# Sums of attention weights by queries, reciprocals transposed to features, and a fused mask and maximum in the first of four blocks

## The chip, the cores and the metric

The kernel runs on one core of a Trainium2 chip, in float32 throughout. The metric is the device time of one execution in microseconds. Five engines work side by side, each through its own instruction queue in order: TensorE (PE; its weight loads are shown as PEld), VectorE (DVE), ScalarE (ACT), GpSimd (POOL) and SyncE (SP), which issues the DMAs. Engines wait for each other through semaphores. Matrix products land in PSUM, of which the kernel uses eight banks of 128 x 512 words in rotation; everything else lies in SBUF.

## The reference, cut to what matters

Four blocks follow each other on x of shape (2, 2048, 256): a grouped-query attention block with its feed-forward part, two layers of a local-attention block, a gated block, and a linear layer with ternary weights. Each is added to its own input. The change lies in the attention of the first block:

```
q = (h @ Wq + bq) in 16 heads of 16;  k, v = 4 heads of 16, each shared by 4 query heads
q, k = rope(q), rope(k)
scores = q k^T / sqrt(16)
valid = (col <= row) & (row - col < 64)      # causal window of 64
attn = softmax(where(valid, scores, -1e9))
x = x + concat_heads(attn @ v) @ Wo + bo
```

Then comes the feed-forward part of the same block, with a layer norm, a product to 1024 features, a gelu and a product back to 256.

## The kernel before, in words

The 4096 rows are 32 tiles of 128 queries, in 8 groups of 4 tiles. A tile goes through the first block in four consecutive steps of a schedule: tile t is projected in step t, scored in step t+1, attended in step t+2 and multiplied by Wo in step t+3. So one step holds four tiles at different stages: `p` (project), `q` (scores), `a` (attend) and `o` (output). The function `step_a` writes out the order by hand, and each engine executes its own instructions in just that order: nothing is reordered.

Groups add work to certain steps. `m` normalises the rows of the group that comes next (line 169, step 4g-2). `n` takes its statistics one step earlier (lines 145 to 159), and in the same steps GpSimd adds the output bias to another group's rows (line 206). `f` prepares the feed-forward part of a finished group (statistics on VectorE, a power on GpSimd at lines 135 and 137, normalised rows at line 197 on VectorE, then eight transposes at line 214 on TensorE); it falls on steps 7, 11, 15, 19, 23, 27, 31 and 35. `e` (last statistics) normalises the finished rows. From step 8 on, the feed-forward products fill the steps: `fill(0)` and `fill(1)` issue two pieces each, either hidden features (lines 555 and 561) or outputs (lines 566 and 573). Steps 2 to 7 attend tiles without such pieces.

The attention of one tile: TensorE makes the scores of 16 heads for a window of 128 keys, 32 small products into four banks (line 449). VectorE adds the mask, a bank of four heads in one operation (`mask`, line 459), takes the maxima of eight heads at a time (`maxima`, line 468), and GpSimd subtracts them (line 469). ScalarE takes the exponents of all 16 heads in one instruction (line 472). In the next step TensorE transposes the weights so that keys lie on partitions (line 479), ScalarE copies them out (line 487), and `values` multiplies them: by V (line 499), and a second time by a matrix of zeros and ones, `one48` (line 506), which gives, for every feature of every head, the sum of that head's weights. `take_values` then takes the reciprocal of 256 columns of sums (line 515) and multiplies (line 516). The program's `ps` tiles are PSUM banks, and nearly all SBUF tiles are slices of one tensor called `room`.

Of the kernel before, what the change touches and what calls it, by code (L numbers as in the profile page):

```python
# [12 lines left out]
ALU = mybir.AluOpType  # L13
AX = mybir.AxisListType
# [3 lines left out]
P = 128  # L18
# [6 lines left out]
KC = D // P  # L25
# [4 lines left out]
AH, AKV, AHD, ADFF, AWIN = 16, 4, 16, 1024, 64  # L30
AKW = AWIN + P
AG = AH // AKV
# [13 lines left out]
def kernel(ctx: ExitStack, tc: tile.TileContext, I: dict, out: bass.AP):  # L46
    nc = tc.nc
    uid = [0]

    def T(pool, shape, tag, bufs=None):  # L50
        uid[0] += 1
        kw = {} if bufs is None else {"bufs": bufs}
        return pool.tile(shape, F32, tag=tag, name=f"{tag}_{uid[0]}", **kw)

    def load(t, src):
        nc.sync.dma_start(out=t, in_=src)
# [9 lines left out]
    small = ctx.enter_context(tc.tile_pool(name="small", bufs=3))  # L66
# [3 lines left out]
    ident = T(const, [P, P], "ident")  # L70
# [9 lines left out]
    def bank():  # L80
        return T(ps, [P, 512], "ps")

    def bank4():
        return bank().rearrange("p (t c) -> p t c", c=P)
# [140 lines left out]
    def load_qkv(l):  # L225
        w = {}
        w["wqkv"] = T(wB, [P, KC, 3 * BIN], "wqkvB")
        load(w["wqkv"], I["L0_ffn_wqkv"][l].rearrange("(k p) n -> p k n", p=P))
        return w
# [42 lines left out]
    wa = Region(HIGH + 5184, W_A, 2, low_tags)  # L272
    ca = wa
# [83 lines left out]
    VW, NVW = 3 * AHD, 4  # L357
# [3 lines left out]
    for i in range(NVW):  # L361
# [3 lines left out]
        for lst, name in ((vown, "vown"), (vmid, "vmid")):  # L365
            lst.append(T(ca, [P, AKV, VW], f"{name}{i}", 1))
            nc.gpsimd.memset(lst[i], 0.0)
    one48 = T(ca, [P, VW], "one48", 1)
    nc.gpsimd.memset(one48, 0.0)
    nc.gpsimd.memset(one48[:, AHD : 2 * AHD], 1.0)  # L370

    class TileA:

# [15 lines left out]
        def take(self):  # L389
            t, tl = self.t, self.t % TPS  # L390
            qkv = self.qkv = T(wa, [P, 384], "qkv")
            nc.vector.tensor_add(qkv, self.pm[:, :384], bqkvA)

            vo = vown[t % NVW]
            nc.gpsimd.tensor_copy(
                vo[:, :, AHD : 2 * AHD], qkv[:, 320:384].rearrange("p (g d) -> p g d", d=AHD)
            )
            load(vmid[t % NVW][64:128], vo[0:64])
            if tl < TPS - 1:
                load(vmid[(t + 1) % NVW][0:64], vo[64:128])  # L400

            nh, hf = AH + AKV, AHD // 2
            qk = self.qk = qkv[:, 0:320].rearrange("p (h d) -> p h d", d=AHD)
            sin = ropeA[:, tl, 1, :].unsqueeze(1)
            t2 = self.t2 = T(wa, [P, nh, AHD], "t2")
            nc.gpsimd.tensor_mul(
                t2[:, :, 0:hf], qk[:, :, hf:AHD], sin[:, :, 0:hf].to_broadcast([P, nh, hf])
            )
            nc.gpsimd.tensor_mul(
                t2[:, :, hf:AHD], qk[:, :, 0:hf], sin[:, :, hf:AHD].to_broadcast([P, nh, hf])  # L410
            )
            cos = ropeA[:, tl, 0, :].unsqueeze(1)
            self.t1 = T(wa, [P, nh, AHD], "t1", 1)
            nc.vector.tensor_mul(self.t1, qk, cos.to_broadcast([P, nh, AHD]))
# [38 lines left out]
                        )  # L453

        def mask(self, g):
            if g == 0:
                self.S = T(wa, [P, AKV * AG, P], "S")
            m = maskA0 if self.first else maskA
            nc.vector.tensor_add(
                self.S[:, g * AG : (g + 1) * AG, :],  # L460
                self.scs[g].rearrange("p (c w) -> p c w", c=AG),
                m.unsqueeze(1).to_broadcast([P, AG, P]),
            )

        def maxima(self, half):
            Sh = self.S[:, half * 2 * AG : (half + 1) * 2 * AG, :]
            mc = T(small, [P, 2 * AG], "mxA")
            nc.vector.reduce_max(mc, Sh, axis=AX.X)
            nc.gpsimd.tensor_sub(Sh, Sh, mc.unsqueeze(2).to_broadcast([P, 2 * AG, P]))  # L469

        def exponents(self):
            nc.scalar.activation(self.S, self.S, AF.Exp, scale=1.0 / AHD**0.5)

        def weights_to_keys(self):
            self.pts = []
# [13 lines left out]

        def values(self):  # L490

            pm = self.po = bank().rearrange("p (s k q) -> p s k q", s=2, k=2)
            vw = (vmid[self.t % NVW], vown[self.t % NVW])
            for b in range(2):
                q = slice(64 * b, 64 * b + 64)
                for e in range(2):
                    c0 = 0 if e else AHD
                    for g in range(AKV):
                        nc.tensor.matmul(
                            pm[32 * g : 32 * g + 32, 0, :, q], vw[b][:, g, c0 : c0 + 32],  # L500
                            self.PT[g // 2][:, g % 2, :, e, q], start=e == 0, stop=e == 1,
                        )
            for e in range(2):
                c0 = 0 if e else AHD
                for g in range(AKV):
                    nc.tensor.matmul(
                        pm[32 * g : 32 * g + 32, 1, :, :], one48[:, c0 : c0 + 32],
                        self.PT[g // 2][:, g % 2, :, e, :], start=e == 0, stop=e == 1,
                    )

        def take_values(self):
            pm = self.po
            self.oT = T(wa, [P, KC, P], "oT")
            rd = T(wa, [P, KC, P], "rdA", 1)
            nc.vector.reciprocal(rd, pm[:, 1])
            nc.vector.tensor_mul(self.oT, pm[:, 0], rd)

        def output(self):
            pm = self.pm = bank()
# [76 lines left out]
    for g in range(NG):  # L596
# [4 lines left out]
        s = GT * (g + 1) + 3  # L601
# [13 lines left out]
    def step_a(todo):  # L615
        p = a = q = o = n = m = f = e = None
        for (g,) in todo.get("load", ()):
            if g:
                groups_a[g] = GroupA(g)
        if "project" in todo:  # L620
            (t,) = todo["project"][0]
            if t == GT:
                weights.update({**load_qkv(0), **load_wo(0), **load_ffn(0)})
            p = tiles_a[t] = TileA(t, groups_a[t // GT])
        if "scores" in todo:
            q = tiles_a[todo["scores"][0][0]]
        if "attend" in todo:
            a = tiles_a[todo["attend"][0][0]]
        if "output" in todo:
            o = tiles_a.pop(todo["output"][0][0])  # L630
        for (g,) in todo.get("residual", ()):
            ffns_a[g] = FfnA(groups_a[g])
        if "statistics" in todo:
            n = groups_a[todo["statistics"][0][0]]
        if "normalise" in todo:
            m = groups_a[todo["normalise"][0][0]]
        if "prepare" in todo:
            f = ffns_a[todo["prepare"][0][0]]
        if "finish" in todo:
            e = ffns_a.pop(todo["finish"][0][0])  # L640

        def fill(place):

            rest = []
            for g, what, i in todo.get(f"fill{place}", ()):
                x = ffns_a[g]
                if what == "hidden":
                    rest.append(lambda x=x, i=i, r=x.hidden(i): x.take_hidden(i, r))
                else:
                    rest.append(lambda x=x, i=i, r=x.output(i): x.take_output(i, r))  # L650
            return rest

        if q:
            q.scores()
            q.mask(0)
            q.mask(1)
        if p:
            p.project()
            p.take()
        if q:  # L660
            q.mask(2)
        if p:
            p.rotate()
        if q:
            q.maxima(0)
            q.mask(3)
            q.maxima(1)
        pieces = fill(0)
        if a and not pieces:
            a.weights_to_keys()  # L670
            a.take_weights()
        for r in pieces:
            r()
        if n:
            n.statistics()
        if f:
            f.statistics()
        if e:
            e.last_statistics()
        if p:  # L680
            p.to_features()
            p.take_features()
        if a and pieces:
            a.weights_to_keys()
            a.take_weights()
        for r in fill(1):
            r()
        if m:
            m.normalise()
        if f:  # L690
            f.normalise()
        if e:
            e.last_normalise()
        if a:
            a.values()
            a.take_values()
        if o:
            o.output()
            o.add_output()
        if q:  # L700
            q.exponents()
        if m:
            m.to_features()
            m.residual()
        if f:
            f.to_features()
        for (g,) in todo.get("bias", ()):
            groups_a[g].add_bias()
# [491 lines left out]
    for l in range(BL):  # L1200
# [9 lines left out]
        for g in range(NG):  # L1210
            s = s0 + GT * (g + 1) + 3
# [511 lines left out]
```

## Time and profile before

| what | value |
| --- | --- |
| median of 3 runs | 2646.41 us (2644.96 to 2647.05) |
| time of the profiled execution | 2644.28 us |
| its span on the core | 2642.5 us |
| granted TensorE clock, mean | 0.99 |
| busy: PE, DVE, ACT, POOL | 97%, 61%, 45%, 38% |
| steps 0 to 34 of the first block | about 4 us to 507 us |

The page gives sums over the whole program, which has several stages with different limits. The first block takes the first fifth of it. A timeline of one engine lists its instructions in order of time: start, duration, engine, line, operation, and in brackets the idle time before it with its releaser. Durations of consecutive VectorE instructions overlap by some 0.08 us, so the distance from start to start, not the duration, says what one more instruction costs. The chain of work that ended last lists, for a stretch of time, the instructions that each instruction in turn was waiting for.

### The profile page before, as it was taken

How to read it: one execution, taken by the hardware profiler on the slowest of the kernel's cores; microseconds unless marked ns; L12 is line 12 of the kernel's file. 1: busy time of each engine (PE TensorE's matmuls, PEld its weight loads, DVE VectorE, ACT ScalarE, POOL GpSimd, SP SyncE). 2: the span in 40 equal slices, each digit the busy share in tenths (PEclk: the TensorE clock that was granted, in tenths of full speed). 3: DMA queues.
4: the chain of work that ended last, by engine and by line, in shares of the span. 5: the costliest groups of instructions: out<-in, count | busy, mean ns of one | idle time of the engine just before them, and what ended most of it. 6: DMA issues, size and time to landing. Idle time of an engine off the chain costs nothing.

```text
span 2642.5 us, 51312 instructions
## 1 busy us (share of the span) xinstructions
PE 2576.2 (97%) x20130; PEld 1645.9 (62%) x20130; DVE 1608.4 (61%) x4357; ACT 1199.7 (45%) x2507; POOL 995.4 (38%) x1237
## 2 busy tenths in 40 slices
PE   6899999998999999999999999999999999999998
PEld 4577777666666666666676676666544455445567
DVE  6878777567666766667666667774434335434344
ACT  3555555465666666756567666663500001500000
POOL 5565555545434544435444445542200002300011
PEclk8999999999999999999999999999999999999999
DMA  5001101111001011011310111101100000100000
GB/s 171 17 31 32 32 32 40 47 33 51 25 17 26 25 26 29 22 55 29 89 37 18 29 34 37 25 22 53 40 8 4 6 7 12 44 0 6 5 11 13
DMA packets 73169, 82.03 MB, mean 31 GB/s; under 512 B 18829, under 2 KB 57056, under 8 KB 72672
## 3 DMA queue, kind: packets, MB, share of 16 engines
q1 hardware_dynamic: 72928, 78.75, 10.6%
q8 instruction: 160, 2.62, 0.4%
q14 instruction: 81, 0.66, 0.1%
HBM read 44.20 MB, written 10.50 MB: 21 GB/s over the span
## 4 chain that ended last, share of the span: by engine, by line
PE 91%; DVE 4%; POOL 3%; issue 1%; DMA 0%; ACT 0%; SPq 0%; POOLq 0%; ACTq 0%; DVEq 0%
PE ps L1576 17%; PE ps L900 12%; PE ps L1154 10%; PE ps L1177 6%; PE ps L1500 4%; PE ps L566 4%; PE ps L555 4%; PE ps L1082 4%; PE ps L975 3%; PE ps L1053 2%; PE ps L1519 2%; PE ps L1488 2%; PE ps L1025 2%; PE ps L956 2%; PE ps L1478 2%; PE ps L479 2%
## 5 line engine op out<-in xcount | busy, mean ns | idle before, releaser
L1576 PE MATMUL ps<-room 128*128 128x512 f32 (+1 forms) x1152 | 463.2, 544 | 0.0
L1576 PEld LDWEIGHTS ps<-room 128*128 128x128 f32 x1152 | 217.8, 189 | 221.9 <-issue 214.7
L900 PE MATMUL ps<-room 128*128 128x512 f32 x768 | 347.4, 602 | 0.0
L1006 ACT ACTIVATE room<-room,shift,rn 128x192 f32<-128x192 f32 x512 | 276.0, 546 | 71.7 <-DVE shift L994 71.7
L921 POOL TENSOR_TENSOR room<-room 128x256 f32<-128x256 f32 x128 | 113.5, 887 | 500.6 <-ACT room L912 500.6
L1154 PE MATMUL ps<-room 128*128 128x512 f32 x640 | 287.6, 593 | 0.4 <-ACT room L219 0.4
L1544 ACT COPY room<-ps 128x256 f32<-128x256 f32 x32 | 11.8, 370 | 587.7 <-PE ps L1542 587.7
L939 POOL TENSOR_TENSOR rn<-ss,mhalf 128x8 f32<-128x8 f32 x128 | 248.2, 1939 | 10.7
L900 PEld LDWEIGHTS ps<-room 128*128 128x128 f32 x768 | 141.0, 190 | 157.8 <-issue 149.9
L1506 DVE SCALAR_TENSOR_TENSOR room<-ps,room 128x512 f32<-128x512 f32 (+1 forms) x144 | 90.1, 626 | 206.5 <-PE ps L1500 206.5
L1154 PEld LDWEIGHTS ps<-room 128*128 128x128 f32 x640 | 118.8, 190 | 137.3 <-issue 131.5
L1529 POOL TENSOR_SCALAR veC<-mvC 128x1 f32<-128x1 f32 x32 | 7.2, 224 | 453.2 <-DVE mvC L1527 453.2
L1177 PE MATMUL ps<-room 128*128 128x256 f32 x768 | 173.0, 379 | 0.0
L987 DVE CUSTOM_DVE_ANT_0 room<-ps,room 128x192 f32<-128x192 f32 x512 | 152.2, 353 | 14.7 <-PE ps L975 14.3
L1177 PEld LDWEIGHTS ps<-room 128*128 128x128 f32 x768 | 143.7, 190 | 24.8 <-issue 6.2
L1017 DVE TENSOR_SCALAR room<-room,rdB 128x192 f32<-128x192 f32 x512 | 151.7, 360 | 4.5
L1170 DVE SCALAR_TENSOR_TENSOR room<-ps,room 128x512 f32<-128x512 f32 x96 | 72.1, 751 | 125.6 <-PE ps L1154 86.8
L469 POOL TENSOR_TENSOR room<-room,mxA 128x1024 f32<-128x1024 f32 x64 | 120.2, 1898 | 58.5 <-PE ps L431 45.4
L936 DVE TENSOR_REDUCE ss<-room 128x8 f32<-128x512 f32 x128 | 81.9, 681 | 94.9 <-ACT room L914 94.9
L1500 PE MATMUL ps<-room 128*128 128x512 f32 (+1 forms) x288 | 133.4, 545 | 0.0
L219 ACT ACTIVATE room<-ps,room 128x512 f32<-128x512 f32 x80 | 58.1, 772 | 143.3 <-PE ps L214 143.0
L1082 PE MATMUL ps<-room 128*128 128x256 f32 x512 | 121.0, 379 | 0.0
(182 smaller groups left out, 5050.1 us busy)
## 6 DMA issues: line engine op xcount, KB each, us to landing
room<-room SPq DMA_DIRECT2D x144, 128.0 KB
room<-in_L_attn_x_dram SPq DMA_DIRECT2D x16, 512.0 KB
room<-in_rope_b_dram SPq DMA_DIRECT2D x16, 512.0 KB
xs<-room SPq DMA_DIRECT2D x8, 512.0 KB
room<-xs SPq DMA_DIRECT2D x8, 512.0 KB
room<-in_rope_c_dram SPq DMA_DIRECT2D x8, 512.0 KB
out_dram<-R SPq DMA_DIRECT2D x32, 128.0 KB
room<-in_L_ffn_w_dram SPq DMA_DIRECT2D x6, 640.0 KB
```

Of the source, the lines that this page charges most:

```text
L469: nc.gpsimd.tensor_sub(Sh, Sh, mc.unsqueeze(2).to_broadcast([P, 2 * AG, P]))
L900: nc.tensor.matmul(pm, src[:, cols], self.w["wqkv"][:, k, part * BIN : (part + 1) * BIN], start=k == 0, stop=k == 1,)
L921: nc.gpsimd.tensor_mul(u2[:, :, 0:hd2], x[:, :, hd2:BHD], sin[:, :, 0:hd2].to_broadcast([P, BH, hd2]))
L939: nc.gpsimd.tensor_tensor(self.rn[part], ss, mhalf[:, 0:BH], ALU.pow)
L987: nc.vector.tensor_tensor_reduce(S[:, e, jj, :], sc[e][:, jj * KW : (jj + 1) * KW], self.mask[:, jj, :], 1.0, -3.0e38, ALU.add, ALU.max, t ...
L1006: nc.scalar.activation(S[:, e, jj, :], S[:, e, jj, :], AF.Exp, bias=self.shift[half][:, a : a + 1], scale=self.rn[0][:, head : head + 1], ...
L1017: nc.vector.tensor_scalar_mul(S[:, e, jj, :], S[:, e, jj, :], rd[:, a : a + 1])
L1082: nc.tensor.matmul(pm[:, 0:D], self.oT[:, k, :], wo[:, k, :], start=k == 0, stop=k == BIN // P - 1)
L1154: nc.tensor.matmul(pm, w["w1"][:, k, half, c * P : (c + 1) * P], hT[:, k, :], start=k == 0, stop=k == KC - 1,)
L1177: nc.tensor.matmul(pm[:, 0:D], hh[:, c, tt * P : (tt + 1) * P], self.w["w2"][:, c, :], start=c == 0, stop=c == BNC - 1,)
L1500: nc.tensor.matmul(pm[:, 0:n], self.KT[:, J * P : (J + 1) * P], self.QT[:, q0 : q0 + n], start=True, stop=True,)
L1576: nc.tensor.matmul(acc[e][:, 0:n], self.V[:, J, e * P : (e + 1) * P], s2, start=J == 0, stop=J == TPS - 1,)
```

## The change

The second product with ones goes. Instead VectorE sums each query's weights, by head, straight from the exponents (`sum_weights`: two sums of eight heads each, a reciprocal of 128 x 16, and two copies that spread each reciprocal over 16 features). TensorE transposes the two spread tiles (`sums_to_features`), ScalarE copies the result out, and `take_values` is left with one multiplication. `values` writes one half of a bank; `sums_to_features` takes one bank more per tile. On the score side, each head is masked and its maximum taken in one operation (`tensor_tensor_reduce`, 16 per tile), and `maxima` becomes `less_maxima`, which only subtracts, on GpSimd as before. In the order of a step, bank 1 is masked after the rotation instead of ahead of the projection, the sums stand on VectorE's queue ahead of the first feed-forward pieces, and the two transposes stand on TensorE's queue just ahead of `values`. The scratch tile `t2` has one buffer instead of two.

```diff
-    one48 = T(ca, [P, VW], "one48", 1)
-    nc.gpsimd.memset(one48, 0.0)
-    nc.gpsimd.memset(one48[:, AHD : 2 * AHD], 1.0)
...
-            t2 = self.t2 = T(wa, [P, nh, AHD], "t2")
+            t2 = self.t2 = T(wa, [P, nh, AHD], "t2", 1)
...
         def mask(self, g):
+
             if g == 0:
                 self.S = T(wa, [P, AKV * AG, P], "S")
+                self.top = T(wa, [P, AKV * AG], "top")
             m = maskA0 if self.first else maskA
-            nc.vector.tensor_add(
-                self.S[:, g * AG : (g + 1) * AG, :],
-                self.scs[g].rearrange("p (c w) -> p c w", c=AG),
-                m.unsqueeze(1).to_broadcast([P, AG, P]),
-            )
-
-        def maxima(self, half):
-            Sh = self.S[:, half * 2 * AG : (half + 1) * 2 * AG, :]
-            mc = T(small, [P, 2 * AG], "mxA")
-            nc.vector.reduce_max(mc, Sh, axis=AX.X)
-            nc.gpsimd.tensor_sub(Sh, Sh, mc.unsqueeze(2).to_broadcast([P, 2 * AG, P]))
+            sc = self.scs[g].rearrange("p (c w) -> p c w", c=AG)
+            for c in range(AG):
+                h = g * AG + c
+                nc.vector.tensor_tensor_reduce(
+                    self.S[:, h, :], sc[:, c, :], m, 1.0, -3.0e38, ALU.add, ALU.max, self.top[:, h : h + 1]
+                )
+
+        def less_maxima(self, half):
+            heads = slice(half * 2 * AG, (half + 1) * 2 * AG)
+            Sh = self.S[:, heads, :]
+            nc.gpsimd.tensor_sub(Sh, Sh, self.top[:, heads].unsqueeze(2).to_broadcast([P, 2 * AG, P]))
...
+        def sum_weights(self):
+
+            sums = T(wa, [P, AKV * AG], "sums", 1)
+            for half in range(2):
+                heads = slice(half * 2 * AG, (half + 1) * 2 * AG)
+                nc.vector.reduce_sum(sums[:, heads], self.S[:, heads, :], axis=AX.X)
+            rd = T(wa, [P, AKV * AG], "rd", 1)
+            nc.vector.reciprocal(rd, sums)
+            rd = rd.rearrange("p (g k e) -> p k g e", g=AKV, k=2)
+            self.rx = T(wa, [P, 2, AKV, 2, AHD], "rx", 1)
+            for k in range(2):
+                nc.vector.tensor_copy(
+                    self.rx[:, k], rd[:, k].unsqueeze(3).to_broadcast([P, AKV, 2, AHD])
+                )
+
+        def sums_to_features(self):
+            pt = bank4()
+            for k in range(2):
+                nc.tensor.transpose(pt[:, k, :], self.rx[:, k], ident)
+            self.rT = T(wa, [P, KC, P], "rT", 1)
+            nc.scalar.copy(self.rT, pt[:, 0:KC, :])
...
-            pm = self.po = bank().rearrange("p (s k q) -> p s k q", s=2, k=2)
+            pm = self.po = bank4()[:, 0:KC, :]
...
-            for e in range(2):
-                c0 = 0 if e else AHD
-                for g in range(AKV):
-                    nc.tensor.matmul(
-                        pm[32 * g : 32 * g + 32, 1, :, :], one48[:, c0 : c0 + 32],
-                        self.PT[g // 2][:, g % 2, :, e, :], start=e == 0, stop=e == 1,
-                    )
-
         def take_values(self):
-            pm = self.po
             self.oT = T(wa, [P, KC, P], "oT")
-            rd = T(wa, [P, KC, P], "rdA", 1)
-            nc.vector.reciprocal(rd, pm[:, 1])
-            nc.vector.tensor_mul(self.oT, pm[:, 0], rd)
+            nc.vector.tensor_mul(self.oT, self.po, self.rT)
...
             q.scores()
             q.mask(0)
-            q.mask(1)
         if p:
             p.project()
             p.take()
...
         if q:
-            q.maxima(0)
+            q.mask(1)
+            q.less_maxima(0)
             q.mask(3)
-            q.maxima(1)
+            q.less_maxima(1)
+        if a:
+            a.sum_weights()
         pieces = fill(0)
...
         if a:
+            a.sums_to_features()
             a.values()
             a.take_values()
```

More of the change, by code (lines that the diff above doesn't have):

```diff
@@ L499, in values @@
                         nc.tensor.matmul(
-                            pm[32 * g : 32 * g + 32, 0, :, q], vw[b][:, g, c0 : c0 + 32],
+                            pm[32 * g : 32 * g + 32, :, q], vw[b][:, g, c0 : c0 + 32],
                             self.PT[g // 2][:, g % 2, :, e, q], start=e == 0, stop=e == 1,
                         )
-            for e in range(2):
-                c0 = 0 if e else AHD
-                for g in range(AKV):
-                    nc.tensor.matmul(
-                        pm[32 * g : 32 * g + 32, 1, :, :], one48[:, c0 : c0 + 32],
-                        self.PT[g // 2][:, g % 2, :, e, :], start=e == 0, stop=e == 1,
-                    )
         def take_values(self):
-            pm = self.po
             self.oT = T(wa, [P, KC, P], "oT")
-            rd = T(wa, [P, KC, P], "rdA", 1)
-            nc.vector.reciprocal(rd, pm[:, 1])
-            nc.vector.tensor_mul(self.oT, pm[:, 0], rd)
+            nc.vector.tensor_mul(self.oT, self.po, self.rT)
         def output(self):
```

## The prediction, made before the changed kernel was run

> **What bounds the kernel now.** I began with the page, whose slices show TensorE nearly full from the third slice on (a slice is 66 us).
>
> ```profile
> PE   6899999998999999999999999999999999999998
> DVE  6878777567666766667666667774434335434344
> ```
>
> A full engine over a slice does not say what happens inside a step, so I read busy times by stretches. The columns are busy microseconds of PE, PEld, DVE, ACT and POOL, with counts.
>
> ```profile
> 50.00:100.00 50.00, 41.43 (x644) 29.35 (x641) 46.64 (x80) 26.28 (x47) 31.00 (x35) 0.97 0.27 84
> 250.00:300.00 50.00, 50.00 (x540) 37.22 (x539) 39.32 (x80) 27.62 (x46) 31.38 (x34) 1.00 0.09 29
> ```
>
> There are two regimes. In steps 3 to 7 VectorE is the busiest engine (46.64 of 50 us). From step 8 on (about 106 us) TensorE never stops, and VectorE idles for a fifth. The chain through a step of the second regime, a prepare step, is all TensorE (start, duration, line):
>
> ```profile
> 218.90 0.44 PE ps L430 x4
> ...
> 221.19 3.46 PE ps L566 x16
> 224.65 1.01 PE ps L499 x32
> 225.66 0.86 PE ps L506 x16
> 226.52 1.06 PE ps L521 x4
> 227.58 0.87 PE ps L214 x8
> 228.45 1.14 PE ps L449 x62
> ```
>
> VectorE in the same step shows how close it runs behind:
>
> ```profile
> 217.66 0.42 DVE L419 TENSOR_TENSOR room<-room 128x256 f32<-128x256 f32 x1 [0.49 <-POOL room L409]
> 218.00 0.22 DVE L424 TENSOR_TENSOR room<-room 128x64 f32<-128x64 f32 x1
> 218.13 1.21 DVE L468 TENSOR_REDUCE mxA<-room 128x8 f32<-128x1024 f32 x1
> 219.26 0.68 DVE L459 TENSOR_TENSOR room<-ps,room 128x512 f32<-128x512 f32 x1
> 219.98 1.22 DVE L468 TENSOR_REDUCE mxA<-room 128x8 f32<-128x1024 f32 x1
> 221.11 0.41 DVE L573 TENSOR_TENSOR room<-ps,room 128x256 f32<-128x256 f32 x1
> ...
> 225.13 2.21 DVE L197 TENSOR_SCALAR room<-room,mv,rs 128x256 f32<-128x256 f32 x4
> 227.26 1.75 DVE L515 RECIPROCAL room<-ps 128x256 f32<-128x256 f32 x1
> ```
>
> Line 197 ends at 227.34, and its fourth row is read by the fourth transpose of line 214, at about 227.58 + 3 x 0.11 = 227.91. VectorE's slack there is 0.57 us. In the first regime the chain alternates between VectorE and GpSimd:
>
> ```profile
> 59.17 0.48 DVE room L392
> 59.70 0.56 POOL room L395
> ...
> 61.81 1.13 DVE mxA L468
> 62.94 0.61 DVE room L459
> 63.58 1.22 DVE mxA L468
> 64.80 1.67 DVE room L515
> ```
>
> **TensorE's saving.** The product with ones goes: 0.86 us in the chain. Two transposes come: four cost 0.44 on line 430, so 0.22. Net -0.64 us for each step that TensorE bounds. Steps 8 to 33 attend tiles with it bound: 26 steps.
>
> **VectorE's pace.** The fused mask and maximum is in the trace already, at line 987, on 192 columns:
>
> ```profile
> 814.43 0.36 DVE L987 CUSTOM_DVE_ANT_0 room<-ps,room 128x192 f32<-128x192 f32 x1 [0.20 <-PE ps L975]
> 814.71 0.08 DVE L987 DVE_READ_ACCUMULATOR2_ANT top<- 128x1 f32 x1
> 814.71 0.35 DVE L987 CUSTOM_DVE_ANT_0 room<-ps,room 128x192 f32<-128x192 f32 x1
> ```
>
> Start to start is 0.28 us, its accumulator read included. Line 468 takes 1.13 us from start to start for 1024 columns and line 459 takes 0.60 for 512: (1.13 - 0.60)/512 = 1.04 ns a column. Then 64 columns fewer save 0.067: 0.213 us a head, 3.4 us for 16, against 4 x 0.60 + 2 x 1.13 = 4.66 before. [...] At the upper bound, the unreduced 0.28, it is 4.5 us.
>
> The sums: two reductions shaped as line 468's, 2 x 1.13 = 2.26, with 0.09 until the last is readable. The reciprocal: 4 columns take 0.168 us at line 1014 and 256 take 1.756 at line 515, so 16 take 0.168 + 12 x 6.3 ns = 0.24. Each copy of 128 columns about 0.2 by the same line of 1.04 ns plus 0.065. Removed at the end: line 515, 1.8 us. The total barely moves (-1.26 + 3.0 - 1.8 = -0.1), but the work moves from behind `values` to ahead of the statistics. That position decides.
>
> **The copies beside GpSimd.** [...] The trace agrees for line 169: four of them last 2.95 us under a subtraction (at 43.39 us) and 1.37 us elsewhere. [...] Unblocked, the two end 0.4 us after the reciprocal; blocked, they wait for the second subtraction. The first starts 0.15 us after bank 1 is masked, and the two take 3.75 us. I take blocked.
>
> **A prepare step afterwards**, from the same 217.66. Rotation until 218.13; banks 1 and 3, eight heads, 1.7 us; sums until 222.3; reciprocal until 222.55. Subtractions: 218.13 + 0.86 + 0.15 + 3.75 = 222.9. Copies until about 223.3. Line 573 started at 221.11 before, so all behind it is d = 2.2 us late (1.85 unblocked): statistics, the power on GpSimd, line 197. TensorE's queue stands still at line 214, and behind it are the next scores and projection. Against before, the step loses 2.2 - 0.57 = 1.6 us, the saving included. Such steps with a tile to attend and TensorE bound are 11, 15, 19, 23, 27 and 31: 6 x 1.6 = +9.7 us. GpSimd's eight additions behind line 197 are late as much, and the next rotation with them, but then TensorE is late too.
>
> The other 20 steps keep their -0.64: -12.8 us. What covers d there: idle VectorE ahead of line 515 or 573 (2.95, 3.16 us) in two steps of the cycle, and in the third 1.47 and 0.32 us of idle, with 0.4 left that the wait for the rotation product takes up. Without that last cover: 6 x 0.5 = 3 us.
>
> **Steps 2 to 7.** Between two projections' additions (59.17 to 68.44) lie 9.27 us. Afterwards: from line 392 to the rotation 2.15 us as before (GpSimd's three operations; the mask of bank 2 fits under them); rotation to copies 0.47 + 1.7 + 2.35 + 0.25 + waiting and copies, 5.6 as above. Then, newly on the path, TensorE: transposes with their latency 0.4, values to the end of the next scores 62.49 to 66.64 less the removed 0.86 = 3.28, projection 1.5. Sum 12.9: +3.7 us, in two such steps +7.4. Step 2: copies at 39.93 + 5.6 = 45.5, where line 169 had ended at 46.3 under GpSimd and now needs 1.4 from 45.5, then values in the way: +1.6. Step 5 (statistics and bias): 7.75 + 2.75 + GpSimd 2.0 + 2.8 + 0.4 + 1.6 = 17.3 against 14.48: +2.8. Step 6: 12.0 against 10.28: +1.75. Step 7, prepare: 7.75 + 2.25 + 1.45 + 3.58 = 15.0 against 12.9: +2.1. Sum +15.7 us.
>
> **Other parts.** ScalarE's copy of 128 x 256 (0.37 us, line 1544) stands ahead of the exponents and cannot run before TensorE's transposes; exponents then end near 211.7 where line 219 was issued at 212.42, now 0.64 earlier: just covered; uncovered 6 x 0.4 = 2.4 us. The extra bank reuses one whose reader is a ScalarE copy long done; bank 3 is released at about 220.0, as before. `t2` with one buffer is free a step ahead; two GpSimd memsets (0.35 us) stand behind loads. No DMA changes.
>
> **Sum.** -12.8 + 9.7 + 15.7 = +12.6 us on the profiled span of 2642.5. The median lies 3.9 above that span, and the change is laid on it: 2646.4 + 12.6 = 2659.0 us.
>
> **Rivals.**
> *A tie.* The prepare steps hide d (TensorE arriving later than I think): 26 x -0.64 = -16.6, with +15.7 in the first steps: 2645.5 us. For it: TensorE waits nowhere in these steps now. Against: 0.57 us of slack and d four times that.
> *Faster.* VectorE's work behind the rotation grows by no more than the slack, because reductions and fused heads run well under their neighbours' rows. Cost changes by 12 us for each us of d (six steps in each regime), so the sign turns at d = 1.1; at 0.57, no prepare loss and about 3.5 us in the first steps: -13, 2633 us. Against: line 468 shows the reduction's price 64 times.
> *Worse.* Fused heads cost 0.28: banks 1 and 3 take 0.55 more in 12 steps, +6.6: 2665.6 us.
>
> **How the numbers follow.** My forecast with the worse variant: 0.80; tie 0.12; faster 0.08. Own range of the forecast: unblocked copies -0.35 x 12 = -4; above it +6.6, or +5.4 from the two thin covers: 2653 to 2667. The range reaches down to 2648 for part of the ties. This kernel's measurement tells 0.2% (5.3 us) from no change; 0.02 of the forecast falls within it: faster 0.08, same 0.14, slower 0.78.
>
> **What would show it.** Right: TensorE waits at line 214 for line 197 in prepare steps by 1.5 to 2.2 us, the chain in steps 3 to 7 runs sums, copies, transposes, values, scores, some 13 us a step; a hidden step near 14.1 us; fused heads 0.21 us apart. Wrong: the step before TensorE's bound begins unchanged, or line 214 finds its rows ready; then the saving stands alone.

## The result, and the profile after

The changed kernel takes 2670.28 us (median of 4 runs, 2668.09 to 2671.77) against 2646.49 us (4 runs, 2644.96 to 2647.05): ratio 1.009, 95% interval 1.0073 to 1.0108. It is slower, by 23.8 us where 12.6 were forecast, and outside the range. Its profiled execution took 2668.09 us with a span of 2666.3 us, so the spans differ by 23.8 us as well.

The slices of the page after the change (TensorE, VectorE, granted TensorE clock in tenths):

```profile
PE   5699999989999999999999999999999999999998
DVE  4778777656667666666666676765433344434344
PEclk7899999999999999999999999999999999999999
```

The clock row of the page before it:

```profile
PEclk8999999999999999999999999999999999999999
```

Apart from dips of a tenth that lie a slice elsewhere, only the first two slices of TensorE and of its clock are lower. The stretches that the prediction showed of before read so after (busy us of PE, PEld, DVE, ACT and POOL with counts, then the granted clock, the DMA share and GB/s):

```profile
50.00:100.00 50.00, 33.84 (x464) 24.78 (x449) 32.31 (x152) 18.73 (x34) 22.17 (x26) 0.78 0.22 65
250.00:300.00 50.00, 50.00 (x547) 35.60 (x545) 39.46 (x190) 30.27 (x47) 27.26 (x37) 1.00 0.10 29
```

From 50 to 100 us every engine is busy for less time than before, VectorE for 32 us instead of 47, and the clock is 0.78 instead of 0.97: this stretch waits, and TensorE is slow in it. Time by place, taken at the first scores behind step 7's transposes of line 214 in the chain: they begin at 106.03 us before (first line) and at 128.05 after (second line), **+22.0 us** (forecast +15.7).

```profile
106.03 1.94 PE ps L449 x64
128.05 1.14 PE ps L446 x63
```

From there to the same place of step 31: 364.40 before, 366.28 after, **+1.9 us** (forecast 6 x (1.6 - 3 x 0.64) = -1.9). Behind step 31: -0.1 (forecast two steps, -1.3).

A light step after the change, from its projection's addition to the next, in the chain (start, duration, line):

```profile
68.16 0.57 DVE room L389
...
70.89 1.69 DVE room L461 x16
72.58 2.27 DVE room L478 x2
...
74.87 0.26 DVE room L480
...
75.16 0.70 DVE room L484 x2
75.86 0.66 PE ps L491 x2
76.52 1.87 PE ps L520 x32
78.39 2.00 PE ps L531 x4
80.39 1.89 PE ps L446 x64
82.28 1.50 PE ps L380 x4
...
83.80 0.57 DVE room L389
```

Line 461 is now the fused head, 478 the sums, 480 the reciprocal, 484 the copies, 491 the transposes of the sums, 520 the values, 531 the output product, 446 the scores, 380 the projection. The order is the forecast one. VectorE's part from the rotation to the end of the copies is 5.53 us (70.33 to 75.86; forecast 5.6). But TensorE needs 75.86 to 83.80 = 7.94 us, where the forecast had 0.4 + 3.28 + 1.5 = 5.18. The clock in this stretch (busy us of TensorE, granted clock, DMA share, GB/s):

```profile
70.00:72.00 2.00, 0.77 (x5) 1.00 0.20 53
...
74.00:76.00 2.00, 0.14 (x1) 0.82 0.00 0
76.00:78.00 2.00, 2.00 (x34) 0.50 0.04 8
...
82.00:84.00 2.00, 2.00 (x24) 0.98 0.00 0
```

TensorE stands idle for more than 4 us while VectorE sums, and then does what waited for it, from the transposes to the scores, at half speed; only the projection is at full speed again.

A prepare step on VectorE after the change (start, duration, line, idle before it):

```profile
237.99 0.42 DVE L416 TENSOR_TENSOR room<-room 128x256 f32<-128x256 f32 x1 [0.25 <-POOL room L406]
...
240.15 2.34 DVE L478 TENSOR_REDUCE room<-room 128x8 f32<-128x1024 f32 x2
...
243.43 0.41 DVE L583 TENSOR_TENSOR room<-ps,room 128x256 f32<-128x256 f32 x1
...
247.44 0.73 DVE L197 TENSOR_SCALAR room<-room,mv,rs 128x256 f32<-128x256 f32 x2 [1.16 <-POOL rs L137]
```

Line 197 begins 9.45 us behind the rotation, 7.47 before: 1.98 us later (forecast 2.2). TensorE waits for it at line 214, here in the step of 309 us:

```profile
306.58 1.13 PE L531 MATMUL ps<-room 128*128 128x256 f32 x4
308.44 0.56 PE L214 MATMUL ps<-ident,room 128*128 128x128 f32 x2 [0.72 <-DVE room L197]
309.40 0.33 PE L214 MATMUL ps<-ident,room 128*128 128x128 f32 x1 [0.40 <-DVE room L197]
310.13 0.77 PE L214 MATMUL ps<-ident,room 128*128 128x128 f32 x5 [0.40 <-DVE room L197]
310.82 2.01 PE L446 MATMUL ps<-room 32*64 32x128 f32 x64
312.76 2.25 PE L380 MATMUL ps<-room 128*128 128x384 f32 x4
```

The waits are 0.72 + 0.40 + 0.40 = 1.5 us, as forecast. The scores behind them take 2.01 us here and 1.21 in the step of 250 us, where the waits are the same.

### The profile page after: what moved, and what is told of

Same layout as the page of the kernel before. It is cut to its first block, busy times and chain, and to the rows that moved or that the text cites. A ratio compares the mean times of both kernels' runs of the same rounds, so it can differ in the third digit from the quotient of the medians.

```text
span 2666.3 us, 51405 instructions
## 1 busy us (share of the span) xinstructions
PE 2573.7 (97%) x19682; PEld 1647.9 (62%) x19682; DVE 1613.8 (61%) x5317; ACT 1209.9 (45%) x2539; POOL 994.4 (37%) x1235
## 4 chain that ended last, share of the span: by engine, by line
PE 88%; DVE 6%; POOL 3%; issue 1%; DMA 0%; ACT 0%; SPq 0%; ACTq 0%; POOLq 0%; DVEq 0%
PE ps L1589 16%; PE ps L913 11%; PE ps L1167 10%; PE ps L1190 6%; PE ps L1513 4%; PE ps L565 4%; PE ps L1095 4%; PE ps L988 3%; PE ps L576 2%; PE ps L1066 2%; PE ps L1532 2%; PE ps L1501 2%; PE ps L1038 2%; PE ps L969 2%; PE ps L380 2%; PE ps L1491 2%
## 5 line engine op out<-in xcount | busy, mean ns | idle before, releaser
L468 POOL TENSOR_TENSOR room<-room 128x1024 f32<-128x1024 f32 x64 | 120.0, 1897 | 48.9 <-DVE room L461 48.9
L461 DVE CUSTOM_DVE_ANT_0 room<-ps,room 128x128 f32<-128x128 f32 x512 | 115.1, 285 | 36.2 <-PE ps L446 36.2
```

The costliest lines, as they stand in the source:

```text
L461: nc.vector.tensor_tensor_reduce(self.S[:, h, :], sc[:, c, :], m, 1.0, -3.0e38, ALU.add, ALU.max, self.top[:, h : h + 1])
L468: nc.gpsimd.tensor_sub(Sh, Sh, self.top[:, heads].unsqueeze(2).to_broadcast([P, 2 * AG, P]))
```

## The experiments

My theory at this point: every wait lies where the prediction put it, and the 11.2 us beyond it are TensorE's clock, which falls where TensorE waits. The rivals: VectorE's new work is dearer than its rows said; the fused heads cost something of their own; the copies and the order of the queue are to blame.

### The fused head alone

```diff
+        def ones(self):
+            return True
...
-        if a:
+        if a and not a.ones():
             a.sum_weights()
...
+                nc.vector.reciprocal(self.rT, self.both[:, 1])
```

Against the changed kernel: every tile keeps the product with ones and the reciprocal of 256 columns; the fused heads and their order stay.

> The fused mask and maximum and its order alone; every tile keeps the product with ones and the reciprocal of 256 columns. My theory (the loss comes from the sums standing on VectorE ahead of other work, and from TensorE's clock in the steps that then wait): TensorE's steps from step 8 on keep their 60.7 us for four, steps 2 to 7 move by less than 1 us each: 2647 us, between 2642 and 2652. Rival (16 small operations a tile in place of 6 large ones are the loss): 2660 us or more.

Measured: 2644.57 us (20 runs) against 2646.62 beside it, ratio 0.9992 (0.9985 to 0.9999): some 2 us faster, which is less than this kernel's measurement tells from no change. The light steps are 9.01 us (9.27 before). Heads follow each other by 0.211 us:

```profile
51.67 0.29 DVE L461 CUSTOM_DVE_ANT_0 room<-ps,room 128x128 f32<-128x128 f32 x1 [3.20 <-PE ps L446]
...
51.88 0.28 DVE L461 CUSTOM_DVE_ANT_0 room<-ps,room 128x128 f32<-128x128 f32 x1
```

(This fence is the changed kernel's timeline of VectorE.) So the loss does not come from the fused heads.

### The sums alone

```diff
-            sc = self.scs[g].rearrange("p (c w) -> p c w", c=AG)
-            for c in range(AG):
-                h = g * AG + c
-                nc.vector.tensor_tensor_reduce(
...
+            nc.vector.tensor_add(
+                self.S[:, g * AG : (g + 1) * AG, :],
...
+        def maxima(self, half):
```

The sums as in the changed kernel; mask, maxima and their order as before.

> The sums by queries alone; masks and maxima as in the kernel before, in its order. My theory: the work behind the rotation on VectorE is then 1.25 us longer (2.96 in place of 1.70 us), in six prepare steps and in six early ones: 2670 + 15 = 2685 us. Rival (the fused operation is the loss): below 2660 us.

Measured: 2697.2 us, ratio 1.0187 (1.017 to 1.0204), about 12 us more than expected. The two parts are not additive (-2.0 and +50.6 against +23.8 together): the fused heads shorten what stands ahead of the sums on VectorE, which by itself is worth next to nothing. Part of the surplus comes through a way that I had not followed. In the steps with the bias, GpSimd waits for late statistics (line 162), then makes four additions (line 206), and the next rotation on VectorE (line 416) and the transposes behind it (line 427) wait for GpSimd. The chain of this kernel there:

```profile
295.19 1.97 POOL rs L162 x2
297.15 3.04 POOL room L206 x4
...
301.36 0.42 DVE room L416
...
301.93 0.63 PE ps L427 x4
```

A cycle of four steps takes about 65.1 us in the middle of the block (60.7 before). VectorE's waits at line 416 for GpSimd sum to 17.6 us between 128 and 494 us (longest 2.3); in the changed kernel they are 6.4 us (longest 0.6). That is not the whole surplus: TensorE's waits at line 214 grow as well (12.6 us in that stretch, 9.2 in the changed kernel), and the clock is lowered to 0.50 in all six prepare steps, where the changed kernel loses it in three. The shares were not told apart.

### TensorE kept busy in steps 2 to 7

```diff
         if a:
+            if a.t < 6:
+                pw = bank()
+                for i in range(4):
+                    nc.tensor.matmul(pw, ident, wf1[:, i % KC, 0:512], start=True, stop=True)
             a.sums_to_features()
```

Four products of 128 x 512 that nobody reads (eight instructions of about 0.5 us in the trace), ahead of the transposes for which TensorE waits.

> The changed kernel, and in steps 2 to 7 four products of 128 x 512 into a bank that nobody reads, just ahead of the transposes of the sums, where TensorE waits for some 3.4 us. My theory (a TensorE that waited works at a lower granted clock, and this doubled the transposes, values, output and scores behind the sums): the work added lies in the wait, those products take 1.0 to 1.1 us each again instead of 1.7 to 2.0, two us less in most of these steps: 2663 us, between 2658 and 2667. Rival (their length has another cause, such as the waits themselves or contention): no shorter, 2670 us or, where the added products are in the way, up to 2685.

Measured: 2664.82 us (2664.14 to 2670.99), ratio 1.0072 (1.0057 to 1.0087). More work on TensorE makes the program 5.5 us faster than the changed kernel by the medians; three of the four runs lie below 2665.3 us, the fourth at 2670.99. The stretch's clock is back at 0.97:

```profile
50.00:100.00 50.00, 41.50 (x499) 26.71 (x500) 37.12 (x177) 21.58 (x41) 25.72 (x29) 0.97 0.24 71
```

and the chain behind the copies runs at the durations that the trace of before shows:

```profile
72.97 0.70 DVE room L484 x2
...
73.67 0.41 PE ps L491 x2
74.08 1.01 PE ps L520 x32
75.09 1.06 PE ps L531 x4
76.16 1.14 PE ps L446 x63
77.29 1.50 PE ps L380 x4
```

From 73.67 to 78.82 are 5.15 us, where the prediction had 5.18 and the changed kernel 7.94. The light step (65.98 to 78.82) is 12.84 us; the prediction's was 12.9. Step 7's mark lies at 122.62: +16.6 us over before, where the changed kernel had +22.0. VectorE's part of the step is the same (5.52 us, 5.53 in the changed kernel). That settles this part: the 5.4 us are the clock, not VectorE's work. Behind the mark nothing is gained: the six cycles take 366.94 us (366.28), with the clock lowered to 0.50 in four prepare steps.

### The product with ones kept in steps 2 to 7

```diff
+        def ones(self):
+            return self.t < 6
...
-            a.sums_to_features()
+            if not a.ones():
+                a.sums_to_features()
```

> The changed kernel, but the six tiles attended in steps 2 to 7 keep the product with ones and their reciprocal; the other 26 have the sums. My theory (22 of the 24 us were lost in these steps): 2649 us, between 2644 and 2654. Rival (each tile carries an equal share of the loss): 2670.3 - 23.8 x 6/32 = 2666 us.

Measured: 2651.14 us (16 runs, 2647.3 to 2658.68), ratio 1.0022 (1.0014 to 1.0031), 2 us over what I expected. The light steps are those of before (9.02 us each), and step 7's mark lies 0.3 us ahead of it. A covered step takes 14.08 us instead of 14.72: the saving of 0.64 us is there to the hundredth. The waits at line 214 remain, and behind them a clock of 0.50 in five prepare steps of six.

### The product with ones kept in the prepare steps too

```diff
+        def ones(self):
+            return self.t < 6 or self.t % GT == 1
```

> The changed kernel, but the tiles attended in steps 2 to 7 and in the prepare steps (every fourth tile) keep the product with ones; 20 tiles have the sums. My theory (outside the waits the sums save TensorE 0.64 us a tile, and the delay hurts in prepare steps alone): 2644.6 - 20 x 0.64 = 2632 us, between 2628 and 2637. Rival (the sums save nothing where TensorE is full, since pipelined products cost less than the chain shows): 2645 us, no change.

Measured: **2633.68 us** (2632.54 to 2635.31), ratio 0.9953 (0.9938 to 0.9967): 12.1 us faster than the kernel before (2645.80 beside it), and the best of all these versions. A middle cycle is 58.78 us (60.71 before), 1.93 less: three covered steps of -0.64. In the profiled execution the six cycles together save 11.3 us (353.09 against 364.39).

### The sums behind the statistics in the prepare steps

```diff
-        if a:
+        if a and not f:
             a.sum_weights()
...
             e.last_statistics()
+        if a and f:
+            a.sum_weights()
```

> The changed kernel, and in prepare steps the sums stand behind the group's statistics on VectorE instead of ahead of them. My theory (statistics, power and normalised rows are late by the sums, and TensorE waits at the transposes of line 214): that wait of 2.2 us becomes one of about 1.0 us ahead of the transposes of the sums, and less of the clock is lost: 2658 us, between 2654 and 2666. Rival (the wait only moves, in full): 2668 to 2672 us.

Measured: 2658.86 us, ratio 1.0049 (1.0032 to 1.0066): 11.4 us faster than the changed kernel with the same work. Line 214 finds its rows ready, TensorE waits 0.57 us for the copies instead, and a cycle is 58.94 us. So in prepare steps it was the place on VectorE's queue that cost, as the prediction said. The loss of the first steps is untouched.

### The copies on ScalarE

```diff
-                nc.vector.tensor_copy(
-                    self.rx[:, k], rd[:, k].unsqueeze(3).to_broadcast([P, AKV, 2, AHD])
-                )
+            self.rd = rd
...
         def sums_to_features(self):
+            for k in range(2):
+                nc.scalar.copy(
```

> The changed kernel, but the two copies that spread the reciprocals run on ScalarE, ahead of the transposes of the sums. My theory (on VectorE they wait for GpSimd's second subtraction and with it hold up the statistics of prepare steps by some 0.7 us): 0.7 us less in six prepare steps, little in steps 2 to 7, where they stay on the way to the transposes: 2665 us, between 2661 and 2669. Rival (the copies are no part of the delay): 2670 us or more.

Measured: 2677.93 us, ratio 1.0117 (1.0102 to 1.0132): a miss, 13 us over what I expected. The prepare step did gain (rotation to line 197 in 8.68 us instead of 9.45), but on ScalarE the copies stood behind the gelus of the second pieces, and TensorE waited for them in the covered steps, which took 15.35 us instead of 14.08. This kernel's chief wait of TensorE from 128 to 494 us (us in total, times, longest):

```profile
PE ps L492 <- ACT room L487: 11.6, 12, 1.0
```

### The same copies, ahead of the second pieces

```diff
+        def spread(self):
             for k in range(2):
-                nc.vector.tensor_copy(
...
             a.take_weights()
+        if a:
+            a.spread()
         for r in fill(1):
```

> The changed kernel, the two spreading copies on ScalarE, now ahead of the second pair of feed-forward pieces on its queue. My theory (with the copies behind that pair's gelus, TensorE waited 1.25 us for them in two steps of four; the prepare step alone gained 0.8 us): the 1.25 us waits go and the gain stays: 2665 us, between 2660 and 2669. Rival (ScalarE's copies delay the transposes wherever they stand): 2674 us or more.

Measured: 2658.81 us (2656.63 to 2659.75), ratio 1.0044 (1.0027 to 1.0061): 19 us better than the version above, so the place on ScalarE's queue was its fault. It is also 6 us better than I expected. The waits at line 214 are 0.40 + 0.40 us, the first one is gone, a cycle is 59.66 us, and the clock does not fall in any of the six prepare steps (1.00 behind each).

### TensorE kept busy ahead of line 214 as well

```diff
         if f:
+            if a:
+                pw = bank()
+                nc.tensor.matmul(pw, ident, wf1[:, 0, 0:512], start=True, stop=True)
             f.to_features()
```

The four products of the third experiment, and one more that nobody reads, 1.02 us in the trace, ahead of line 214.

> As the kernel with four products in steps 2 to 7 into a bank that nobody reads, and one more such product ahead of line 214 in each prepare step that attends a tile, where TensorE waits for some 1.6 us. My theory (a wait at line 214 also lowers the clock granted in the next scores and projection, 1 to 1.5 us in four of six prepare steps): 2664.8 - 4 = 2661 us, between 2658 and 2664. Rival (the clock matters in steps 2 to 7 alone): 2665 us or more.

Measured: 2658.49 us (2656.57 to 2661.07), ratio 1.0046 (1.0031 to 1.0061), 12.7 us over the kernel before beside it. The prediction's sum was +12.6; the table below compares the two by place. A prepare step on TensorE:

```profile
300.51 0.56 PE L214 MATMUL ps<-ident,room 128*128 128x128 f32 x2
301.47 0.33 PE L214 MATMUL ps<-ident,room 128*128 128x128 f32 x1 [0.41 <-DVE room L197]
302.20 0.77 PE L214 MATMUL ps<-ident,room 128*128 128x128 f32 x5 [0.40 <-DVE room L197]
302.90 1.21 PE L446 MATMUL ps<-room 32*64 32x128 f32 x64
304.04 1.56 PE L380 MATMUL ps<-room 128*128 128x384 f32 x4
```

The first wait is filled, the others remain, and the scores are at full speed (1.21 us, a clock of 1.00), in all six prepare steps. The cycles are 60.45 us each but for the last; in the changed kernel they are 60.89, 61.52, 60.43, 62.42, 61.45 and 59.57. The mark of step 7 lies at 121.56, +15.5 us (forecast +15.7).

## When the clock falls

In the changed kernel's first block the granted clock, read finely, is 1.00 or 0.50, and its changes lie on a grid: in prepare steps it falls at 187.90, 310.78 and 372.22 us, 36 and 18 times 3.413 us apart, and stays low for one such interval (187.90 to 191.32 us). Cut along this grid, TensorE's busy time and the granted clock of the intervals at three prepare steps and of those that follow:

```profile
184.49:187.90 3.41, 1.87 (x8) 1.00 0.38 154
187.90:191.32 3.42, 3.42 (x70) 0.50 0.00 0
245.93:249.34 3.41, 2.22 (x19) 1.00 0.40 159
249.34:252.76 3.42, 3.07 (x73) 1.00 0.00 0
307.37:310.78 3.41, 1.88 (x10) 1.00 0.40 159
310.78:314.20 3.42, 3.42 (x68) 0.50 0.00 0
```

An interval with 1.87 us of recorded work is followed by half the clock, one with 2.22 is not; the waits are the same, only the grid lies differently over them. The other three steps fit: 1.87 lowered, 2.21 and 2.43 not. In the kernel of the third experiment 1.87, 2.05, 1.88 and 1.88 us were followed by half the clock, 2.26 and 2.29 were not. In the kernel that keeps ones early, 1.87 to 1.90 were (five steps), 2.30 was not. In the two that had line 214's last two waits alone (copies on ScalarE ahead of the second pieces; TensorE kept busy at both places), none of these six steps lost its clock, and the emptiest interval at each had 2.60 us or more.

Recorded work is not the measure itself. In the early steps of the changed kernel an interval with 1.93 us, sixteen transposes with one pause of 0.95 us among them, is not followed by half the clock; the empty interval behind it is (0.50 from 105.98 us on):

```profile
99.16:102.57 3.41, 1.93 (x16) 1.00 0.11 29
102.57:105.98 3.41, 0.00 (x0) 1.00 0.00 0
```

A transpose that stands alone is recorded with 0.27 us, while eight of line 214 without waits take 1.04 us together, so they follow each other every 0.11 us: where line 214 waits, the records overstate the work. If each product is counted only until the next could start, an estimate from these spacings gives some 1.1 us, a third of the interval, for the changed kernel's three lowered steps, 1.3 to 1.5 for its other three, and 1.6 for the sixteen transposes. This is no sharp bound: in the kernel that keeps ones early an interval with 2.16 us of recorded work (from 1307.93 us) was followed by half the clock, and with the sums alone one with 2.07 us (from 520.08 us).

So the clock also falls behind intervals in which TensorE was not idle: in the lowered prepare steps of the changed kernel and of the third experiment it worked in 55% to 60% of the interval by the records (1.87 to 2.05 us of 3.413), in those of the changed kernel in about a third by the estimate. Three of the changed kernel's six prepare steps lost their clock, for +4.4 us (the six cycles take 366.28 us, and 361.88 in the version that keeps TensorE busy at both places).

## Why the prediction was right or wrong

- **TensorE's saving**, -0.64 us a covered step: right, 14.72 to 14.08.
- **Fused head**, 0.213 us: right, 0.211 from start to start.
- **Sums and reciprocal**, 2.26 + 0.09 and 0.24: right, 2.34 and 0.25. (The prediction's end of the sums, 222.3, adds up to 222.2 from its own terms; the subtraction's end, from which it goes on, is not touched by that.)
- **Copies blocked by GpSimd's second subtraction**: the end is right (5.6 us behind the rotation, measured 5.51 and 5.53). Single copies take 211 to 1931 ns. With the sums alone, where they come after the subtraction, the median is 226 ns; in the changed kernel it is 550. The longest lasts as long as a subtraction (1.9 us). What makes a copy last that long was not tested apart.
- **Prepare steps**, d = 2.2 and 1.6 us lost: right in mechanism and place, 1.98 us late and 1.5 us of waits; an undisturbed cycle is 60.43 us, where 60.73 + 1.6 - 3 x 0.64 = 60.41 was forecast. So the covers that the prediction called thin held. Not foreseen were the three windows at half the clock behind them, +4.4.
- **Steps 2 to 7**, +15.7: the sequence is right, the size is not, +22.0. The failed step is "values to the end of the next scores 62.49 to 66.64 less the removed 0.86 = 3.28, projection 1.5". These durations come from a step in which TensorE idled for 0.74 us at most at a time, while in the predicted order TensorE waits for more than 4 us for the copies. In a light step, behind such a wait, values to scores took 5.76 us (76.52 to 82.28), and the two transposes ahead of them 0.66 instead of 0.41. The projection kept its 1.50. With the clock kept up values to scores took 3.21, and steps 2 to 7 came to +15.5.
- **Range**: its upper end stood on dearer heads (0.28). A lower clock was in no bound, though the trace of before had its price: line 214's transposes there take 272 to 476 ns, and the one at 103.97 us, of 0.47 us, ran at a granted clock of 0.50.
- **Behind step 31**: -0.1 where -1.3 was forecast. To the products behind step 35's transposes it is -0.9; the other +0.8 lies behind them, where the change has no instruction.

By place, in the profiled executions, against the kernel before (us; step 35 ends with the first product behind its transposes of line 214):

| place | forecast | changed kernel | TensorE kept busy at both places |
| --- | --- | --- | --- |
| to step 7's mark | +15.7 | +22.0 | +15.5 |
| from there to step 31's | -1.9 | +1.9 | -2.5 |
| from there to the end of step 35 | -1.3 | -0.9 | -1.3 |
| behind step 35 | 0 | +0.8 | +4.7 |
| whole span | +12.6 | +23.8 | +16.4 |

Up to step 35, where the change lies, the changed kernel loses 23.0 us, and 11.7 with TensorE kept busy, where the forecast's terms sum to 12.5. So some 11.3 us are the clock: 6.5 in steps 2 to 7, 4.4 in the cycles and 0.4 behind. Of the -2.5 in the second row, 1.0 is the first cycle of the kernel before, which itself ran in part at a lowered clock (0.50 from 106 to 108 us; 61.70 us, 60.7 in each of the next four). That the medians, 2658.49 measured and 2659.0 forecast, lie so close is partly luck: the profiled execution, at 2661.07 us the slowest of its four, lost 4.7 us behind step 35, and what the others lost there is not known.

Of the rivals, the tie is excluded by the waits at line 214, the faster one by d, and the worse one by the heads' 0.211 us. A fourth, that the clock falls where the change makes TensorE wait, was missing.

## What to carry to other kernels

Where a change makes TensorE wait in a place where it did not, count the products behind the wait at half speed as well (here 5.76 us at a granted clock of 0.52 for what took 3.21 at 1.00), and read their price from a row in which TensorE had waited. Work moved from TensorE to VectorE pays in the steps that TensorE bounds and costs in those where it waits for VectorE; the choice can be made tile by tile, and doing so turned +23.8 us into -12.1. A short wait can be dearer than its length: 1.5 us of waits at line 214 let the clock fall in three steps of six, the 0.8 us that were left without the first of them did in none.

## What the runs showed of the hardware that was not expected

- The clock fell after stretches that were not idle (55% to 60% by the records, about a third by the estimate above), and whether it did depended on where a grid of 3.413 us lay over the same waits. The version with ones kept early varies from 2647.3 to 2658.7 us from run to run; its runs up to 2651.23 us have a mean granted clock of 0.985 to 0.987, those from 2654.39 on 0.982 to 0.984. The prepare steps alone do not explain that. In the one of these executions that has a trace (2658.68 us, five of six prepare steps lowered), 5.1 of the 14.4 us over the kernel before lie up to the end of step 35 and 9.3 behind it, where the clock falls seven times (three times in the kernel before) ahead of the program's last 10 us. That the grid falls differently over the waits of the later blocks as well would explain the spread; this is argued, not shown.
- Products that nobody reads made the program faster: four of them in each of steps 2 to 7 brought 5.5 us by the medians, 5.4 of them up to step 7's mark in the trace.
